# Spectral layer on one core: one subtraction, one set of stores, the exponentials and the interleaves of a spectrum placed elsewhere

## Chip, core and metric

The kernel runs on one core of one Trainium2 chip. The metric is device time in microseconds (us) of one execution, given as the median of several runs. Engines are named as in the profile: PE is TensorE, DVE is VectorE, ACT is ScalarE, POOL is GpSimd and SP is SyncE, which here only issues DMAs. Every engine works through its own queue in order.

## What is computed

The input x is 16 images of 16 channels, 256x256, fp32. Layer 0 normalises it by groups, applies a pole-residue operator (a convolution through the 2-D Fourier transform plus a transient part made of exponentials) and adds the result to x. Layer 1 normalises again, applies an involution network with a 3x3 convolution, and gates. The change touches layer 0 alone:

```python
alpha = jnp.fft.fft2(x, axes=(-2, -1))                   # x here is the normalised input
A = 1.0 / (omega1[:, None, None, None] - weights_pole1[None])
Bm = 1.0 / (omega2[:, None, None, None] - weights_pole2[None])
S = jnp.einsum('ikpq,oikp,xikq->oxik', weights_residue, A, Bm)
output_residue1 = jnp.einsum('biox,oxik->bkox', alpha, S)
C = jnp.einsum('biox,oikp->bikpx', alpha, A)
D = jnp.einsum('bikpx,xikq->bikpq', C, Bm)
output_residue2 = jnp.einsum('bikpq,ikpq->bkpq', D, weights_residue)
x1 = jnp.fft.ifft2(output_residue1, s=(Ny, Nx), axes=(-2, -1)).real
E1 = jnp.exp(weights_pole1[..., None] * tyc)             # complex exponentials
E2 = jnp.exp(weights_pole2[..., None] * txc)
F = jnp.einsum('kbpq,bipz->kbiqz', output_residue2, E1)
x2 = jnp.einsum('kbiqz,biqx->kizx', F, E2).real
return x1 + x2 / Nx / Ny
```

## The kernel before

Four stages run one after the other: `layer0_forward`, `layer0_mix`, `layer0_back`, `layer1`. Intermediate arrays go through DRAM: `al` (the spectrum), `hd`, `zn` and tables `td`, `avd`, `ed`.

**Forward** takes 64 steps, one for each image b and each group cg of four channels. `fetch` (L156) loads four planes `z` (1 MB) on SP, takes their statistics on DVE (L166, L168), and forms the even part (a sum, L172, DVE) and the odd part (a difference, L171, POOL) of the two halves of each image. `halves` (L175) applies the norm and folds the other axis (L185 to L191, DVE); `group_norm_scalars` sits between, with small DVE steps and a square root on ACT (L46). `rows` (L195) multiplies on PE by the Fourier matrix (L204) and by the pole table `at` (L211); ACT evicts (L218, L223). `poles` (L226) multiplies by the table `bt` (L233), and DVE and POOL accumulate (L244, L257 to L259). `columns` (L294) transforms the other axis for the image before: two PSUM tiles of matmuls (L305), two ACT evictions into a tile `o` (L312), and four stores of `o` to `al` issued from POOL (L321), twice a step; `o` has two buffers. After the 64 steps the columns of the last image remain.

`at` and `bt` are built at the start by `table` (L120), each in two halves of eight channels, with two 3.3 us reciprocals on DVE in each half: `at` whole before the first `rows`, `bt` whole during step 0. `tables` (L377) builds three more tables for the later stages. It is a generator: the step loop calls `next(pieces)` at L352 and L360, and what is left runs after the loop (L361). Its last part (L507 to L543) makes the exponentials of both axes: for each axis and each pair of channels it scales the coordinate by the poles' imaginary parts (L520), reduces the angle, takes the sine on ACT (L528), scales by the real parts (L531), runs `exponential` (a polynomial on DVE, L829) over 128x512, multiplies both (L535), and stores to `ed` from SP. The real parts of one axis fill 64 partitions; here they stand twice.

In this stage only PE's order is that of the program text. The other queues are ordered when the program is built, from its readiness estimates, so table work is spread over the steps.

**Mix** has 33 groups g. All its compute engines run in the order of the text. Each group holds four rounds f of `columns` for the group before (PE L733, ACT L743, then DVE L746, L747, L752 and POOL L753) and `mix` (PE L698, reading the spectrum tile `alb`), and then eight `residues` (PE L679; evicted by ACT L690 and DVE L688 in turn) between three `turn`s (PE L714). `columns` of one round cannot start on PE before DVE has emptied its two PSUM tiles of the round before (L746, L747). The next spectrum is brought in eight pieces q: SP loads one into one of two buffers `alc` (L599), and `interleave` (L631) writes it on DVE into the single tile `alx` (L628, L629) and then lets SP load the next piece. When all eight are in, `ends` fixes two rows, and `place` (L649) copies `alx` to `alb` by four DMAs of 512 KB (L652) once the last `mix` has been done. `poles` (L663) runs in round 1. Pieces 2 to 7 are interleaved in rounds 0 to 2, two in each, `ends` follows in round 2, and pieces 0 and 1 of the group after come behind the last residues.

Of the kernel before, what the change touches and what calls it, by code (L numbers as in the profile page):

```python
# [71 lines left out]
def layer0_forward(ctx, tc, d, al, bd, tabs):  # L72
# [31 lines left out]
    op = ctx.enter_context(tc.tile_pool(name="fo", bufs=2))  # L104
# [9 lines left out]
    def table_inputs(axis):  # L114
        wx = ap.tile([P, 2, 3, P], F32, tag="wx", name="wx")
        nc.sync.dma_start(out=wx, in_=d["wx"])
        w = frequencies(nc, ap, d["ty" if axis == "1" else "tx"], kcol, [P, 2], f"w{axis}")
        return wx, w

    def table(axis, wx, w):  # L120

        t, planes = (at, (0, 1)) if axis == "1" else (bt, (1, 2, 0))
        for half in range(2):
            cols = slice(512 * half, 512 * half + 512)
            pr = ap.tile([P, 512], F32, tag="pr", name="pr")
            pi = ap.tile([P, 512], F32, tag="pi", name="pi")
            nc.sync.dma_start(out=pr, in_=d[f"p{axis}r"][:, cols].to_broadcast([P, 512]))
            nc.sync.dma_start(out=pi, in_=d[f"p{axis}i"][:, cols].to_broadcast([P, 512]))
            p2 = ap.tile([P, 512], F32, tag="p2", name="p2")
            nc.gpsimd.tensor_tensor(p2, pr, pr, ALU.mult)  # L130
            q = ap.tile([P, 2, 2, 512], F32, tag="q", name="q", bufs=2)
            for h in range(2):
                e, r = q[:, h, 1], q[:, h, 0]
                nc.vector.tensor_scalar(e, pi, -1.0, w[:, h : h + 1], ALU.mult, ALU.add)
                nc.vector.tensor_tensor(r, e, e, ALU.mult)
                nc.vector.tensor_tensor(r, r, p2, ALU.add)
                nc.vector.reciprocal(r, r)
                nc.vector.scalar_tensor_tensor(e, e, -1.0, r, ALU.mult, ALU.mult)
                nc.vector.scalar_tensor_tensor(r, pr, -1.0, r, ALU.mult, ALU.mult)

            for y in range(2):
                for out, terms in ((0, ((0, 0), (2, 1))), (1, ((0, 1), (1, 0)))):
                    ps = psx.tile([P, 512], F32, tag="px", name="aps")
                    for n, (trig, part) in enumerate(terms):
                        nc.tensor.matmul(
                            ps, lhsT=wx[:, y, trig], rhs=q[:, y, part], start=n == 0, stop=n == 1
                        )
                    dst = t[:, y, 8 * half : 8 * half + 8]
                    src = ps.rearrange("p (c m) -> p c m", m=64)
                    nc.scalar.copy(dst[:, :, planes[out]], src)  # L150
                    if out and len(planes) == 3:
                        nc.vector.tensor_scalar(dst[:, :, planes[2]], src, -1.0, None, ALU.mult)
# [3 lines left out]
    def fetch(b, cg):  # L156
# [5 lines left out]
        )  # L162
        mv = sm.tile([P, 2, 2], F32, tag="mv", name="mv")
# [7 lines left out]
        nc.gpsimd.tensor_tensor(parts[:, 1], z[:, :, 0], z[:, :, 1], ALU.subtract)  # L171
        nc.vector.tensor_tensor(parts[:, 0], z[:, :, 0], z[:, :, 1], ALU.add)  # L172
        return eo, mv
# [120 lines left out]
    def columns(b, g0, rsc):  # L294
# [23 lines left out]
        for k in range(min(2, n)):  # L318
            w = (n - k + 1) // 2
            for v in range(2):  # L320
                nc.gpsimd.dma_start(  # L321
# [6 lines left out]
    with tc.manual_schedule(engines={mybir.EngineType.PE}):  # L328
        args = table_inputs("1")
        fetched = [fetch(*steps[0]), fetch(*steps[1])]  # L330
        table("1", *args)
# [3 lines left out]
        for i, (b, cg) in enumerate(steps):  # L335
            now, following = ready, iter(())
# [11 lines left out]
            if i == 0:  # L348
                table("2", *table_inputs("2"))
                passing.close()  # L350
# [1266 lines left out]
```

## Time and profile before

| what | value |
|---|---|
| runs of the kernel before | 6137.18, 6151.72, 6154.14 us; median 6151.72 us |
| profiled execution | 6126.97 us, of which the span (first to last instruction) is 6125.2 us |
| busy over the span | PE 5614.2 us (92%), DVE 4802.4 us (78%), POOL 2928.5 us (48%), ACT 2264.7 us (37%) |
| forward | 0 to about 1230 us; steps in 60 to 1167 us, then the last image's columns |
| mix | about 1230 to 2365 us |
| back and layer 1 | the rest |

Times in the profile are counted from the start of the span. The page splits the span into 40 slices of 153 us each, so forward is the first eight digits of each row and mix the next seven or so. A row of the timeline gives start, duration, engine, line, operation, tiles written and read, and in brackets the engine's idle time before and what ended it. Consecutive DVE instructions overlap: 128x128 instructions of 0.38 us start 0.22 us apart. In rows of waits the columns are total us, how often, and the longest.

### The profile page before, as it was taken

The page shows a single profiled execution, that of the slowest core. Times are in us where ns is not written, and L with a number is a line of the kernel's source. Part 1 is how long each engine was busy: PE and PEld are TensorE (multiplying, and loading weights), DVE is VectorE, ACT ScalarE, POOL GpSimd, SP SyncE. Part 2 cuts the span into 40 slices and gives each one's busy share as a digit, 9 for nine tenths or more (in the row PEclk, how much of TensorE's full clock was granted, in tenths as well). Part 3 has the DMA queues.
Part 4 walks back from the last instruction along what each step waited for, and adds up shares of the span by engine and source line. Part 5 has one row for each costly group of instructions (what it writes and reads, how often), then busy time and mean ns, then how long its engine had stood idle before and what let it go on. Part 6 is the DMA issues. An engine that isn't in the chain of part 4 may idle for free.

```text
span 6125.2 us, 217025 instructions
## 1 busy us (share of the span) xinstructions
PE 5614.2 (92%) x94280; PEld 3210.1 (52%) x94280; DVE 4802.4 (78%) x9275; ACT 2264.7 (37%) x4076; POOL 2928.5 (48%) x4154
## 2 busy tenths in 40 slices
PE   6888888778888887999899999999999999999997
PEld 4788888756776766777633333333333333333332
DVE  8999998767777775888828777778777787777784
ACT  2333444434434443222233333333333433333332
POOL 2455555523333333666633554445544455544453
PEclk9999999889999999999989999999999999999998
DMA  3445444456556566999867888888888888888886
GB/s 94 138 139 149 140 134 132 123 182 197 183 184 196 186 195 210 323 326 328 294 180 229 269 266 250 251 279 276 266 245 246 262 275 272 264 246 249 276 268 230
DMA packets 814779, 1370.51 MB, mean 224 GB/s; under 512 B 140001, under 2 KB 629345, under 8 KB 798689
## 3 DMA queue, kind: packets, MB, share of 16 engines
q1 hardware_dynamic: 596480, 882.02, 45.5%
q0 software_dynamic: 217344, 474.61, 25.2%
q8 instruction: 741, 12.14, 0.8%
q14 instruction: 214, 1.75, 0.1%
HBM read 730.18 MB, written 556.47 MB: 210 GB/s over the span
## 4 chain that ended last, share of the span: by engine, by line
PE 62%; DVE 12%; DMA 3%; issue 2%; ACT 1%; POOL 1%; SPq 0%; DVEq 0%; ACTq 0%; POOLq 0%
PE pd L1166 15%; PE c2ps L1244 15%; PE c L1116 12%; PE ps L679 4%; PE ph L733 3%; PE pr L1144 2%; DVE planes L1235 2%; PE pt L714 2%; PE py L923 2%; PE pg L698 2%; PE py L924 2%; DMA alc<-al 2%; DVE zb L955 1%; DVE st L940 1%; DVE alx L628 1%
## 5 line engine op out<-in xcount | busy, mean ns | idle before, releaser
L1196 POOL DMA_DIRECT2D cf<-top x1152 | 667.9, 692 | 1151.9 <-DVE top L1183 1011.7
L1235 DVE TENSOR_TENSOR planes<-rows 128x1152 f32<-128x1152 f32 x960 | 1201.1, 1293 | 0.0
L1166 PE MATMUL pd<-wide,dw 32*32 32x512 f32 x27648 | 1029.7, 601 | 28.0 <-issue 13.7
L1125 ACT ACTIVATE bot<-c,b 128x512 f32<-128x512 f32 x576 | 364.9, 684 | 1445.8 <-PE c L1116 1091.4
L1116 PE MATMUL c<-z,w 18*64 18x512 f32 x13824 | 833.5, 602 | 16.9 <-DMA z<-zn 16.9
L1166 PEld LDWEIGHTS pd<-wide,dw 32*32 32x32 f32 x27648 | 446.7, 103 | 588.5 <-issue 449.8
L1181 DVE TENSOR_TENSOR t<-pd,r 128x512 f32<-128x512 f32 x576 | 357.6, 683 | 479.8 <-PE pd L1166 479.8
L1116 PEld LDWEIGHTS c<-z,w 18*64 18x64 f32 x13824 | 291.1, 132 | 533.9 <-issue 411.9
L753 POOL TENSOR_TENSOR h<-w 128x256 f32<-128x256 f32 x258 | 193.6, 750 | 641.0 <-DVE w L747 638.1
L1214 POOL DMA_DIRECT2D cf<-bot x720 | 394.9, 619 | 217.8 <-DMA cf<-top 100.5
L1244 PE MATMUL c2ps<-planes,c 128*32 128x512 f32 x3968 | 477.5, 598 | 0.0
L1183 DVE TENSOR_TENSOR top<-pd,t 128x512 f32<-128x512 f32 x576 | 357.7, 683 | 100.0 <-PE pd L1166 99.6
L936 POOL TENSOR_TENSOR x<-x,o 128x512 f32<-128x512 f32 x256 | 324.0, 1266 | 215.6 <-DVE o L935 214.2
L204 PE MATMUL pu<-fy,f 128*128 128x128 f32 x2048 | 408.5, 281 | 7.9 <-ACT u L218 7.9
L1341 POOL TENSOR_SCALAR o<-o,scale,mean 128x258 f32<-128x258 f32 x488 | 341.5, 707 | 151.2 <-DVE scale L1333 132.0
L321 POOL DMA_DIRECT2D al<-o x544 | 337.4, 627 | 128.1 <-ACT o L312 83.6
L211 PE MATMUL pv<-at,f 128*128 128x128 f32 x2048 | 397.5, 276 | 0.0
L733 PE MATMUL ph<-ix,yt 64*128 64x128 f32 x4128 | 320.9, 298 | 73.0 <-DVE w L747 65.2
L1133 ACT ACTIVATE wide<-c,b 128x512 f32<-128x512 f32 x576 | 365.0, 693 | 0.0
L305 PE MATMUL px<-wxn,u 128*128 128x128 f32 (+1 forms) x2176 | 313.5, 306 | 42.2 <-ACT tt L441 24.1
L688 DVE COPY s<-ps 128x1024 f32<-128x1024 f32 x132 | 161.7, 1225 | 233.5 <-PE ps L679 233.5
L733 PEld LDWEIGHTS ph<-ix,yt 64*128 64x128 f32 x4128 | 286.0, 205 | 108.0 <-issue 82.4
(240 smaller groups left out, 10468.6 us busy)
## 6 DMA issues: line engine op xcount, KB each, us to landing
rows<-cf SPq DMA_DIRECT2D x128, 2176.0 KB
cf<-top POOLq DMA_DIRECT2D x896, 112.0 KB, 5.7
cf<-bot POOLq DMA_DIRECT2D x336, 224.0 KB, 6.3
z<-zn SPq DMA_DIRECT2D x576, 129.0 KB
alb<-alx SPq DMA_DIRECT2D x132, 512.0 KB
zn<-zb SPq DMA_DIRECT2D x128, 516.0 KB
o<-zn SPq DMA_DIRECT2D x128, 516.0 KB
z<-in_x SPq DMA_DIRECT2D x64, 1024.0 KB
```

The costliest lines, as they stand in the source:

```text
L204: nc.tensor.matmul(pu[:, h, :, :, e].rearrange("p v g m -> p (v g) m"), lhsT=f[:, e, c, h], rhs=fy[:, e].rearrange("p (n m) -> p n m", m=2 ...
L211: nc.tensor.matmul(pv[:, a, h], lhsT=f[:, e, c, h], rhs=at[:, e, 4 * cg + c].rearrange("p l m -> p (l m)"), start=e == 0, stop=e == 1,)
L733: nc.tensor.matmul(ph[q][:, e, blocks], lhsT=yt[lanes, i].rearrange("p t k -> p (t k)"), rhs=ix[lanes, i].rearrange("p (b x) -> p b x", b= ...
L1116: nc.tensor.matmul(ps[half, a][to : to + 64], lhsT=w1[lanes, dx], rhs=self.z[lanes, c : c + 2, dx : dx + N], start=dx == 0, stop=dx == 2,)
L1125: nc.scalar.activation(self.bot[:, c : c + 2], ps[1, a].rearrange("p c (x e) -> p c e x", e=2)[:, :, ::-1], AF.Mish, bias=b1[1],)
L1133: nc.scalar.activation(self.feat[:, c : c + 2, 1 : N + 1], ps[0, a], AF.Mish, bias=b1[0])
L1166: nc.tensor.matmul(out[32 * k : 32 * k + 32], lhsT=dw[lanes, kernel, dx], rhs=self.feat[lanes, 2 * k : 2 * k + 2, dx : dx + N], start=dx == 0,
L1183: nc.vector.tensor_tensor(self.top[:, s, half], out, t, ALU.add)
L1196: nc.gpsimd.dma_start(out=rows[y + 2 * lo : y + 2 * hi, :, c + 2 * k : c + 2 * k + 2].rearrange("y f c x -> y f (c x)"), in_=o[32 * k + 2 ...
L1214: nc.gpsimd.dma_start(out=rows[y + 4 * lo : y + 4 * hi, to : to + n].rearrange("p c x -> p (c x)"), in_=src.rearrange("p c q x -> p (c q x)"),
L1235: nc.vector.tensor_tensor(planes[:, k, rows], x[:, rows], y[:, rows], op_)
L1244: nc.tensor.matmul(ps[32 * j : 32 * j + 32], lhsT=w[:, blk], rhs=src[:, 4 * j + blk : 4 * j + blk + 4], start=(i, blk) == (0, 0), stop=(i, ...
```

## The change

1. Forward, `fetch`: the difference L171 goes from POOL to DVE. The load of `z` becomes a function of its own, `bring`, called at the top of a step for two steps ahead instead of at its end.
2. Forward, `columns`: the four stores a tile go from POOL to SP; `o` gets three buffers instead of two.
3. Forward, `table`: called by halves. Half 0 of `at` comes before the first step, half 0 of `bt` in step 0, both halves 1 in step 2. `wx` is loaded once instead of twice.
4. `tables`, exponentials: one `exponential` of 128x512 for both axes and two channels (axis 1 in partitions 0 to 63, axis 2 in the others), so 8 instead of 16. ACT makes its arguments and a copy with the halves exchanged; ACT also scales the angles (formerly L520). The product with the sine is done by halves of 64 partitions, for axis 2 together with the scale `last` (formerly L534). 24 pieces instead of 32.
5. Mix, `spread`: two instructions of 128x256 instead of four of 128x128 for a piece.
6. Mix, order: pieces 0 and 1 come behind residues 4 and 5, pieces 2 and 3 behind the last residues, 4 in round 0, 5 and 6 in round 2, 7 and `ends` in round 3, ahead of that round's copy L806.

`layer0_back` and `layer1` are not touched (`exponential` gets a parameter for a buffer's tag).

```diff
-    op = ctx.enter_context(tc.tile_pool(name="fo", bufs=2))
+    op = ctx.enter_context(tc.tile_pool(name="fo", bufs=3))
...
-    def table(axis, wx, w):
+    def table(half, axis, wx, w):
 
         t, planes = (at, (0, 1)) if axis == "1" else (bt, (1, 2, 0))
-        for half in range(2):
-            cols = slice(512 * half, 512 * half + 512)
...
+        cols = slice(512 * half, 512 * half + 512)
...
-    def fetch(b, cg):
+    def bring(b, cg):
 
         z = xp.tile([P, 4, 2, N], F32, tag="z", name="z")
         nc.sync.dma_start(
             out=z.rearrange("p c h x -> p (c h) x"),
             in_=d["x"][b, 4 * cg : 4 * cg + 4].rearrange("c (h p) x -> p (c h) x", p=P),
         )
+        return z
+
+    def fetch(z):
+
...
-        nc.gpsimd.tensor_tensor(parts[:, 1], z[:, :, 0], z[:, :, 1], ALU.subtract)
         nc.vector.tensor_tensor(parts[:, 0], z[:, :, 0], z[:, :, 1], ALU.add)
+        nc.vector.tensor_tensor(parts[:, 1], z[:, :, 0], z[:, :, 1], ALU.subtract)
         return eo, mv
...
-                nc.gpsimd.dma_start(
+                nc.sync.dma_start(
                     out=al[g0 // 2 + k, :, v, :, b, :w].rearrange("h c g x -> h c (g x)"),
...
-        args = table_inputs("1")
-        fetched = [fetch(*steps[0]), fetch(*steps[1])]
-        table("1", *args)
+        w1 = table_inputs("1")
+        wx = load(nc, ap, d["wx"], [P, 2, 3, P], "wx")
+        zs = [bring(*steps[0]), bring(*steps[1])]
+        table(0, "1", wx, w1)
+        fetched = [fetch(zs.pop(0)), fetch(zs.pop(0))]
+        w2 = table_inputs("2")
...
         for i, (b, cg) in enumerate(steps):
             now, following = ready, iter(())
+            if i + 2 < len(steps):
+                zs.append(bring(*steps[i + 2]))
+            if i == 2:
+                table(1, "1", wx, w1)
...
-            if i == 0:
-                table("2", *table_inputs("2"))
+            if i in (0, 2):
+                table(i // 2, "2", wx, w2)
+            if i == 2:
                 passing.close()
...
             if i + 2 < len(steps):
-                fetched.append(fetch(*steps[i + 2]))
+                fetched.append(fetch(zs.pop(0)))
...
+    for k in range(0, C, 2):
+        grown = tp.tile([P, 2, N], F32, tag="grown", name="grown")
+        for j in range(2):
+            for i, tr in enumerate(trs):
+                own = slice(64 * i, 64 * i + 64)
+                nc.scalar.activation(
+                    grown[own, j], tr[own], AF.Copy, scale=pr[own, k + j : k + j + 1]
+                )
+        exponential(nc, tp, grown.rearrange("p k x -> p (k x)"), "arg")
+        other = tp.tile([P, 2 * N], F32, tag="exp_n", name="other").rearrange("p (k x) -> p k x", k=2)
+        nc.scalar.copy(other[64:], grown[:64])
+        nc.scalar.copy(other[:64], grown[64:])
+        yield
+        for i in range(2):
...
             for j in range(2):
-                nc.vector.tensor_scalar(arg[:, j], tr, pi[:, k + j : k + j + 1], None, ALU.mult)
+                nc.scalar.activation(arg[:, j], trs[i], AF.Copy, scale=pis[i][:, k + j : k + j + 1])
...
-            yield
-            for j in range(2):
-                nc.vector.tensor_scalar(arg[:, j], tr, pr[:, k + j : k + j + 1], None, ALU.mult)
-            exponential(nc, tp, af)
-            if axis == "2":
-                nc.vector.tensor_scalar(n, n, last, None, ALU.mult)
-            nc.vector.tensor_tensor(arg, arg, n, ALU.mult)
-            if axis == "1":
+            for a, e in ((i, grown), (1 - i, other)):
+                own = slice(64 * a, 64 * a + 64)
+                if i:
+                    nc.vector.scalar_tensor_tensor(
+                        arg[own], n[own], last[own], e[own], ALU.mult, ALU.mult
+                    )
+                else:
+                    nc.vector.tensor_tensor(arg[own], n[own], e[own], ALU.mult)
+            if i == 0:
...
-        for h in range(2):
-            a, b = src[:, :, h, 0], src[:, :, h, 1]
-            nc.vector.tensor_tensor(dst[:, :, h, 0], a, b, ALU.add)
-            nc.vector.tensor_tensor(dst[:, :, h, 1], b, a, ALU.subtract)
+        a, b = src[:, :, :, 0], src[:, :, :, 1]
+        nc.vector.tensor_tensor(dst[:, :, :, 0], a, b, ALU.add)
+        nc.vector.tensor_tensor(dst[:, :, :, 1], b, a, ALU.subtract)
...
         alx = new_spectrum()
-        for q in range(2):
+        for q in range(4):
             interleave(alx, q)
...
-                if more and f < 3:
-                    for q in (2 + 2 * f, 3 + 2 * f):
+                if more:
+                    for q in ((4,), (), (5, 6), (7,))[f]:
                         interleave(alx, q)
-                    if f == 2:
+                    if f == 3:
                         ends(alx)
...
-                    if f == 3 and g + 2 < NF:
-                        for q in range(2):
+                    if f >= 2 and g + 2 < NF:
+                        for q in (2 * f - 4, 2 * f - 3):
                             interleave(alx, q)
```

## The prediction

> **What bounds it now.** I read the row of busy tenths first, then sums by stage, then the waits of forward, then single steps in the timeline.
>
> ```profile
> DVE  8999998767777775888828777778777787777784
> PEclk9999999889999999999989999999999999999998
> ```
>
> DVE is full through the first six slices, which are forward. The sums by stage (engine busy us, then clock, DMA share, GB/s):
>
> ```profile
> core 0: us, PE busy (x) PEld busy (x) DVE busy (x) ACT busy (x) POOL busy (x), PEclk, DMA share, GB/s
> 100.00:1167.00 1067.00, 943.42 (x8694) 883.66 (x8693) 1004.06 (x2366) 446.17 (x748) 568.73 (x749) 0.96 0.47 134
> 131.60:161.90 30.30, 28.39 (x280) 26.81 (x277) 30.27 (x83) 11.98 (x21) 14.49 (x17) 1.00 0.47 140
> 1262.00:2330.00 1068.00, 933.39 (x28406) 750.69 (x28398) 802.61 (x2078) 431.10 (x695) 353.60 (x480) 0.96 0.59 188
> ```
>
> In the 62 forward steps from 100 to 1167 DVE works 94% of the time, and PE 88%. The third row is two steps almost without table work. In mix (fourth) PE leads, and no engine is full. Waits in forward:
>
> ```profile
> ACT gnr L46 <- DVE gnv L44: 144.1, 42, 6.4
> PE pd L233 <- ACT v L223: 76.1, 41, 4.9
> ACT o L312 <- DMA al<-o: 40.2, 14, 5.5
> ```
>
> ACT stands at L46 until DVE has the variance; L223 stands behind it in ACT's queue, and PE waits for L223. So DVE sets the pace, by way of ACT. And L312 waits for a free buffer `o` once an image. One step shows what holds DVE up:
>
> ```profile
> 513.79 2.84 DVE L50 TENSOR_TENSOR gnt<-gnr 128x2 f32<-128x2 f32 x1
> 514.23 2.37 POOL L171 TENSOR_TENSOR eo<-z 128x1024 f32<-128x1024 f32 x1
> 516.55 0.28 DVE L485 TENSOR_TENSOR ar<-ar,tpr 128x128 f32<-128x128 f32 x1
> ```
>
> A two-element-wide DVE op (0.15 us elsewhere) lasts 2.84 us and ends as POOL's difference ends: DVE stands still for the whole of L171.
>
> **Difference to DVE.** L171 goes: 64 x 2.37 = 152 us in which DVE is held. Added: 64 x 1.22 (L172's median, same shape) = 78. Net -74 if DVE is always held. At the other end only two lines' excess counts: L50 64 x (0.73 - 0.15) = 37, L172 64 x (1.69 - 1.22) = 30, so 67 - 78 = +11. Other two-input lines have long ones too (L845 up to 3.86 against 0.69), so I take -70.
>
> The Trainium skill (Perfetto Trace Analysis, Optimizing Scalar/DVE Operations) says that a saturated DVE may be relieved by giving work to Scalar or even GPSIMD, which speaks against this edit; it adds that those two share a read port, so that this might not help. By the first half alone DVE would get 78 us more and forward would grow by about that; the rows above show the second half.
>
> **Exponentials.** One `exponential` takes 9.0 us of DVE (its 14 instructions where they ran alone, 1185.7 to 1195.2). Eight fewer: -72. L520 and L531 go to ACT: 16 x 2 x 0.62 = -20. L534 goes: 8 x 0.48 = -4. L535 becomes two of half the partitions, each as long (0.69): +11. Net -85. Some 8 of it lie behind 1167, so -77 in the steps. ACT gets 8 x (8 x 0.375 + 2 x 0.59) = 33 us (L743's 128x256, L718's 128x512), and it is idle over half the time. But each pair of channels now has six places where ACT, in order, waits for low-priority DVE work, against two before. 24 more, at 0.5 us (L528 waited 8.2 us in 16) to 3 us: 12 to 72 us on ACT, with evictions L218 and L223 behind. PE sees part of it: I take 17.
>
> **The 62 steps.** DVE after: 1004 - 70 - 77 = 857. PE: 943 busy less at most 4% of 1067 lost to the clock (0.96), 900. So PE becomes the bound. In the two plain steps PE was busy 28.39 of 30.30, 0.937: 900 / 0.937 = 960, a gain of 107, less 17 = **-90**. Bounds: -164 - 3 (PE never waits) and -25 (the difference gains nothing and ACT's new waits eat most of the rest).
>
> **Stores on SP, third buffer.** 8.5 stores a step leave POOL (0.63 us each, hidden there already) for SP, at 0.33 (table store L497) to 0.77 us (L652): 3 to 7 us of a 15 us step, SP being nearly empty. They now stand in order with loads of `z` and stores of `td`, `avd`, `ed`, which wait for DVE; before, they stood behind POOL's sums, which also wait for DVE. Behind a late one stand L312, then L218; three buffers cover 1.5 steps. Loads of `z` come a step early, so little waits for them. I cost this at nothing; the 40 us of L312's waits are inside the -90.
>
> **After the steps.** From 1167 to the last landing at about 1228 the last image's 17 evictions wait for stores again and again, and one left-over exponential sits among them.
>
> ```profile
> 1167.00:1262.00 95.00, 46.06 (x507) 37.28 (x509) 44.51 (x75) 20.54 (x29) 37.52 (x49) 0.72 0.54 171
> 1181.06 0.68 ACT L312 ACTIVATE o<-px,rsc 64x512 f32<-64x512 f32 x1 [6.51 <-DMA al<-o]
> 1212.78 1.27 ACT L312 ACTIVATE o<-px,rsc 128x512 f32<-128x512 f32 x2 [5.86 <-DMA al<-o]
> ```
>
> 61 us now. With 73 pieces (81 before) against 80 calls, none is left over. 8.25 tiles of 512 KB at mix's 188 GB/s are 23 us, PE's part 17, and a landing 5 more: 28 to 36. **-25** (-5 to -33).
>
> **Tables by halves.** The work stays; PE may run steps 1 and 2 (21 us between 99.5 and 120.5) while DVE makes the second halves, but DVE is 93% busy from 15.6 to 99.5. Between 0 and -21: **-12**.
>
> **Mix, spread.** Merging looks like a saving of two instructions' overhead, but rows of both shapes exist:
>
> ```profile
> 1244.90 0.58 DVE L628 TENSOR_TENSOR alx<-first 128x256 f32<-128x256 f32 x1
> 1245.33 0.59 DVE L629 TENSOR_TENSOR alx<-first 128x256 f32<-128x256 f32 x1
> 1261.29 0.38 DVE L628 TENSOR_TENSOR alx<-alc 128x128 f32<-128x128 f32 x1 [8.87 <-DMA alb<-alx]
> 1261.51 0.38 DVE L629 TENSOR_TENSOR alx<-alc 128x128 f32<-128x128 f32 x1
> ```
>
> Starts lie 0.43 and 0.22 us apart: a piece is 0.87 or 0.88. Nothing.
>
> **Mix, order.** One group now, about 35.0 us on average, 35.6 here:
>
> ```profile
> 1717.92 4.96 DMA alc<-al
> 1724.71 1.87 DVE L663 TENSOR_TENSOR lt<-av,m 128x512 f32<-128x512 f32 x3
> 1727.39 0.46 PE L733 MATMUL ph<-ix,yt 64*128 64x128 f32 x2 [2.59 <-DVE w L747]
> 1728.06 3.55 PE L733 MATMUL ph<-ix,yt 64*128 64x128 f32 x30 [0.20 <-DVE w L747]
> 1733.59 4.62 SPq L652 DMA_DIRECT2D alb<-alx  x4
> 1734.21 0.69 DVE L806 COPY y<-pg 128x512 f32<-128x512 f32 x1
> ```
>
> In round 1 DVE waits for pieces 4 and 5 (a pair of loads takes 5.0 us), then makes L663, and only then L747, for which PE waits 2.6 us. That stall goes. A new one comes. Count from L806, when the copy to `alb` is also issued. Residue 5 is copied by 9.0 (1.95 to the first DVE residue copy, twice 2.92, 1.23). Piece 0 needs `alx` free: 8.8 (1252.49 to 1261.29) to 10.4 us (median by the packets). Pieces 0 and 1 end at 10.8 to 12.2; the load for piece 2 starts after piece 0 and lands at 14.8 to 16.2; pieces 2 and 3 end at 16.6 to 18.0; the four L746/L747 (1.32) at 17.9 to 19.3. Only then can PE start round 1, which starts at 16.5 now (1715.16): **+1.4 to +2.8**. From there to the next L806 it is 19.05 now. New: round 3 starts on PE after 9.5 (four PE pieces of 1.95, two small waits); L752, pieces 5 and 6, one POOL clash, L746/L747, L752, piece 7, `ends` take 7.0, and 1.5 more if piece 7's load is late: 16.5 to 18.4, **-2.6 to -0.7**. Together -1.2 to +2.1 against this group, some 0.6 more against the mean: +1.0 x 32 = **+32** (-19 to +86).
>
> After the 2.6 us stall the clock was half from 1727.9 to 1731.3, and the next 1.98 us of matmul took 3.55. I leave that inside both sums, as the new stall is about as long. The Trainium skill (TensorE: Matmul & The Clock Gate, Part 1) wants an idle window of about 3.4 us for the lower clock; by it stalls this short would cost none, 1.6 us a group less, an estimate of some 50 us for the stage.
>
> **Sum.** -90 - 12 - 25 + 32 = -95. The profiled execution, 6127.0, becomes 6032. The median, 6151.7, lies 25 above it; the same on top gives **6057**.
>
> **Rivals.**
> 1. *PE-bound throughout* (0.13): forward's steps reach PE's 900 us, the stall in mix merely moves. -164 - 15 - 28 + 0 = -207: 5945. For it: two steps without columns have PE busy 19.9 of 21.0 us. Against: normalisation still crosses three engines a step.
> 2. *The queues take it back* (0.15): ACT behind the new exponential steps or SP behind table stores keeps DVE's old pace. -30 - 5 - 20 + 20 = -35: 6117. For it: L46's 144 us show how ACT's order costs PE. Against: three buffers, and half of ACT free.
> 3. *Slower* (0.14): the chain `alb` copy, piece 0, load, piece 2 in mix. With the copy at 10.4, the load at 5.0 and one POOL clash, round 1 starts at 20.3, +3.8; if late piece 7 also eats the gain behind it, 32 x 3.8 = +122, against a forward at its poor end, -60 - 5 - 25 = -90: +32, 6184. It decides from a loss of 2.8 us a group at that forward. Against: round 3's stall does go.
> My forecast has 0.58, its own range 5990 to 6125.
>
> **Chances.** Measurement cannot tell less than 0.3%, 18 us. Faster: 0.58 + 0.13 + half of rival 2 = 0.78; same 0.08; slower 0.14. Range 5975 to 6150.
>
> **What would show it.** Right: in forward DVE near 88% busy, PE near 92%, no DVE op of 2 us and more, steps of 15.8 us on average (977 / 62; 17.2 now); the time from the last step to `alb`'s memset near 36 us; in mix PE waiting for L747 in round 1 instead of round 3, and DVE waiting for `alc` ahead of piece 2. Wrong: ACT waiting for L846 or L527 by tens of us, SP waiting long with L312 waiting for `al<-o`, or groups of mix over 37 us.

## Result, and the profile after

The changed kernel takes 6169.78 us (median of 12 runs, 6154.98 to 6190.41), the kernel before 6152.32 us on the same chip (12 runs). The ratio is 1.0035, with a 95% interval of 1.0018 to 1.0051: about 21 us slower, where 95 us less had been forecast. The profiled execution takes 6178.25 us (span 6176.5), 51 us more than the profiled one of before. More than half of that is chance: the execution profiled before lies 25 us under its median, this one 8 us over its own.

The rows of busy tenths of the changed kernel, then its sums by stage (columns as in the prediction). The first stage runs from the second of the 64 steps to the end of the last. The prediction calls this stretch 62 steps; it holds 63 (2016 of the 2048 matmuls of L204, 32 a step).

```profile
DVE  8878778377777775888827777788777787777784
PEclk9999999899999998999989999999999999999998
```

```profile
core 0: us, PE busy (x) PEld busy (x) DVE busy (x) ACT busy (x) POOL busy (x), PEclk, DMA share, GB/s
67.70:1171.70 1104.00, 971.85 (x8734) 902.13 (x8732) 878.10 (x2324) 499.81 (x840) 110.38 (x189) 0.95 0.40 130
1171.70:1264.40 92.70, 41.16 (x479) 33.13 (x477) 22.25 (x25) 19.69 (x28) 9.07 (x5) 0.77 0.42 151
1264.00:2406.00 1142.00, 954.18 (x29312) 758.93 (x29312) 875.19 (x1637) 446.52 (x718) 382.36 (x496) 0.96 0.58 182
```

VectorE has been relieved as intended: 878 us busy in the 63 steps instead of 1004. Yet the steps take 1104 us instead of 1068, TensorE is busy for 88% of them as before, and the clock is no better. So something that is no engine's own work holds them. The waits in the 63 steps say where to look:

```profile
DVE st L167 <- DMA z<-in_x: 134.9, 44, 7.1
ACT gnr L46 <- DVE gnv L44: 101.6, 32, 6.7
PE gn_var L42 <- DVE gnq L39: 75.0, 30, 4.5
```

VectorE, which waited 10 us in all for the loads of `z` before, now waits 135 us for them. What stands behind the statistics in its queue is late, so L46's wait is still there, and TensorE now waits 75 us for the variance (11.5 before). The step that the prediction looked at (VectorE's timeline):

```profile
517.79 1.22 DVE L172 TENSOR_TENSOR eo<-z 128x1024 f32<-128x1024 f32 x1
518.92 1.22 DVE L173 TENSOR_TENSOR eo<-z 128x1024 f32<-128x1024 f32 x1
520.93 0.15 DVE L50 TENSOR_TENSOR gnt<-gnr 128x2 f32<-128x2 f32 x1
531.63 2.47 DVE L167 BATCH_NORM_STATS2 st<-z 128x6 f32<-128x512 f32 x4 [4.80 <-DMA z<-in_x]
```

L50 has gone from 2.84 to 0.15 us, and the difference L173 costs its 1.22 us. Ten us later VectorE stands still for 4.8 us because `z` has not landed. By the packets a load of `z` takes 7.5 us from issue to last packet (median), against 5.0 before. Its first packet ends 1.1 us after the issue in both kernels, and seven eighths of its packets have ended after 5.4 us (4.4 before): it is the tail that comes late. After the rows, ScalarE's timeline shows one eviction of `o` after another:

```profile
1203.80 1.27 ACT L313 ACTIVATE o<-px,rsc 128x512 f32<-128x512 f32 x2 [3.80 <-DMA al<-o]
1209.02 1.27 ACT L313 ACTIVATE o<-px,rsc 128x512 f32<-128x512 f32 x2 [3.95 <-DMA al<-o]
1214.09 1.27 ACT L313 ACTIVATE o<-px,rsc 128x512 f32<-128x512 f32 x2 [3.80 <-DMA al<-o]
```

A tile of 512 KB leaves every 5.1 us, although there are three buffers now. The view of the DMA queues, from 1196 to 1224 us (packets and rate; then queue, packets, MB, share of 16 engines):

```profile
DMA packets 1477, 2.87 MB, mean 102 GB/s; under 512 B 87, under 2 KB 87, under 8 KB 1475
...
q1 hardware_dynamic: 1475, 2.84, 26.2%
```

With nothing else to do, the stores move 102 GB/s and use 26.2% of sixteen engines, that is 4.2. The stretches of the profiled pair add up: the second step starts 31.8 us earlier (67.7 instead of 99.5), the steps take 36.0 more, the time from the last matmul of the rows to the first copy into `alb` 7.6 more (92.6 instead of 85.0), mix's 32 groups 31.6 more, and the rest, which is not touched, 7.8 more.

### The profile page after: what moved, and what is told of

Read it like the earlier page. It is cut to its first block, busy times and chain, and to the rows that moved or that the text cites. A ratio compares the mean times of both kernels' runs of the same rounds, so it can differ in the third digit from the quotient of the medians.

```text
span 6176.5 us, 216287 instructions
## 1 busy us (share of the span) xinstructions
PE 5616.6 (91%) x94280; PEld 3210.0 (52%) x94280; DVE 4678.7 (76%) x8643; ACT 2310.8 (37%) x4158; POOL 2451.4 (40%) x3546
## 4 chain that ended last, share of the span: by engine, by line
PE 51%; DVE 8%; issue 1%; DMA 1%; POOL 1%; ACT 0%; SPq 0%; DVEq 0%; ACTq 0%; POOLq 0%
PE pd L1193 15%; PE c2ps L1271 15%; PE c L1143 12%; PE pr L1171 2%; DVE planes L1262 2%; PE py L950 2%; PE py L951 2%; DVE zb L982 1%; DVE st L967 1%; PE pf L939 1%; DVE o L962 1%; DVE top L1210 0%; DVE o L961 0%; PE gn_mean L34 0%; ACT odd L959 0%
## 5 line engine op out<-in xcount | busy, mean ns | idle before, releaser
L1193 PE MATMUL pd<-wide,dw 32*32 32x512 f32 x27648 | 1033.3, 600 | 30.4 <-issue 15.5
L780 POOL TENSOR_TENSOR h<-w 128x256 f32<-128x256 f32 x258 | 210.3, 815 | 669.4 <-DVE w L774 663.3
L205 PE MATMUL pu<-fy,f 128*128 128x128 f32 x2048 | 430.5, 294 | 5.0 <-ACT u L219 5.0
L212 PE MATMUL pv<-at,f 128*128 128x128 f32 x2048 | 417.8, 288 | 0.0
L706 PE MATMUL ps<-tt,lt 64*32 64x256 f32 x8448 | 297.5, 405 | 111.7 <-DVE y L833 78.1
L725 PE MATMUL pg<-alb,s 128*32 128x64 f32 x16896 | 284.5, 222 | 67.0 <-issue 47.1
L205 PEld LDWEIGHTS pu<-fy,f 128*128 128x128 f32 x2048 | 334.0, 205 | 7.0 <-ACT u L219 5.9
L212 PEld LDWEIGHTS pv<-at,f 128*128 128x128 f32 x2048 | 333.0, 204 | 0.0
L306 PE MATMUL px<-wxn,u 128*128 128x128 f32 (+1 forms) x2176 | 289.6, 291 | 47.7 <-ACT o L313 31.2
```

Of the source, the lines that this page charges most:

```text
L205: nc.tensor.matmul(pu[:, h, :, :, e].rearrange("p v g m -> p (v g) m"), lhsT=f[:, e, c, h], rhs=fy[:, e].rearrange("p (n m) -> p n m", m=2 ...
L212: nc.tensor.matmul(pv[:, a, h], lhsT=f[:, e, c, h], rhs=at[:, e, 4 * cg + c].rearrange("p l m -> p (l m)"), start=e == 0, stop=e == 1,)
L1193: nc.tensor.matmul(out[32 * k : 32 * k + 32], lhsT=dw[lanes, kernel, dx], rhs=self.feat[lanes, 2 * k : 2 * k + 2, dx : dx + N], start=dx == 0,
```

## Experiments

Four questions: which part of the change takes forward's gain away; is it SyncE's queue or the engines that its stores run on; what is each other term worth; and what costs in mix. The table gives, from each profiled execution, the start of the second step, the length of the 63 steps from there on, TensorE's and VectorE's share in them, the time from the last matmul of the rows to the first copy into `alb`, and the mean group of mix. Ratios are to the kernel before on the same chip. A single profiled execution can lie well off its kernel's median (before 25 us under it, e3 20 and e7 13 us over), so differences of 10 or 20 us between profiles alone show little.

| kernel | median us | ratio, 95% | second step | 63 steps | PE, DVE | after the rows | group |
|---|---|---|---|---|---|---|---|
| before | 6152.32 | 1 | 99.5 | 1068.0 | .88, .94 | 85.0 | 34.98 |
| changed | 6169.78 | 1.0035, 1.0018 to 1.0051 | 67.7 | 1104.0 | .88, .80 | 92.6 | 36.03 |
| e1_stores_pool | 6068.32 | 0.9881, 0.9860 to 0.9903 | 67.5 | 1023.7 | .92, .86 | 70.6 | 35.90 |
| e2_mix_old | 6153.99 | 1.0016, 1.0003 to 1.0029 | 67.6 | 1085.2 | .89, .81 | 92.6 | 35.63 |
| e3_only_stores_sp | 6178.73 | 1.0060, 1.0038 to 1.0082 | 101.9 | 1088.9 | .87, .86 | 102.9 | 35.55 |
| e4_stores_pool_mix_old | 6062.48 | 0.9862, 0.9842 to 0.9882 | 66.5 | 1014.2 | .92, .87 | 73.5 | 35.78 |
| e5_z_on_pool | 6184.73 | 1.0051, 1.0034 to 1.0068 | 66.4 | 1105.3 | .88, .80 | 91.6 | 36.35 |
| e6_stores_by_16 | 6498.61 | 1.0558, 1.0535 to 1.0581 | 67.0 | 1389.6 | .75, .66 | 121.3 | 36.09 |
| e7_only_sub_dve | 6077.57 | 0.9885, 0.9866 to 0.9904 | 101.5 | 1005.5 | .93, .88 | 83.3 | 35.61 |
| e8_only_mix_new | 6185.52 | 1.0063, 1.0044 to 1.0082 | 99.1 | 1071.5 | .88, .94 | 85.1 | 36.31 |
| e9_sp_c_first | 6026.36 | 0.9810, 0.9792 to 0.9828 | 68.7 | 981.2 | .94, .90 | 66.2 | 35.94 |
| e10_sp_c_first_mix_old | 6018.32 | 0.9799, 0.9782 to 0.9816 | 68.0 | 976.3 | .94, .91 | 64.6 | 35.88 |
| e11_exp_old | 6077.58 | 0.9893, 0.9875 to 0.9911 | 67.7 | 1024.7 | .93, .89 | 83.7 | 35.91 |
| e12_only_sp_c_first | 6059.83 | 0.9856, 0.9835 to 0.9877 | 100.2 | 985.7 | .93, .95 | 74.0 | 35.42 |
| e13_mix_new_copy_first | 6148.60 | 1.0009, 0.9998 to 1.0021 | 99.2 | 1070.2 | .89, .94 | 88.2 | 35.41 |
| e14_sp_c_first_copy_first | 6019.21 | 0.9801, 0.9781 to 0.9822 | 69.1 | 979.4 | .94, .90 | 64.7 | 36.06 |

### Which part takes the gain

Two parts of the change were undone, alone and together, and one was made alone in the kernel before.

```diff
 e1, e4 (in the changed kernel)
-                nc.sync.dma_start(
+                nc.gpsimd.dma_start(
                     out=al[g0 // 2 + k, :, v, :, b, :w].rearrange("h c g x -> h c (g x)"),
 e2, e4 (in the changed kernel: mix's old order)
-        for q in range(4):
+        for q in range(2):
...
 e3 (in the kernel before)
-                nc.gpsimd.dma_start(
+                nc.sync.dma_start(
```

> The changed kernel with its spectrum stores (al<-o) issued from GpSimd again; the third buffer o stays. Theory A (the stores on SP are what eats forward's gain: they run on 4 of the 16 DMA engines at 102 GB/s, and the loads of z stand behind them in one queue, 8.0 us instead of 5.0 from issue to last packet, so that DVE waits 135 us for z): the waits of DVE for z fall under 30 us, the last rows matmul of forward comes at 1060 to 1100 us instead of 1172, the time from there to the first copy to alb falls from 93 to 60 to 70 us; in all 90 to 140 us less than the changed kernel, ratio to the kernel before 0.98 to 0.99. Rival B (ACT's new exponential steps and the fixed order of DVE's queue hold forward up): within 25 us of the changed kernel.

> The changed kernel with the old places of the interleaves and of ends in mix (the merged spread stays). Theory A (the new order trades the stall in round 3 for a longer one in round 1): groups of mix return from 36.0 to 35.0 us, 33 us less in all, about 0.998 of the kernel before. Rival B (the 1.05 us a group are scatter or come from the merged spread): groups stay at 36 us, no change.

> The kernel before with one edit: the stores of al issued from SP; two buffers o as before. Theory A (4 engines, z behind the stores): DVE's waits for z rise from 10 to 60 us and more, the last columns take 20 us longer or more; 40 to 100 us slower than the kernel before. Rival B: no change beyond 15 us.

> Both of the first two: stores from GpSimd and the old order in mix, all else as in the changed kernel. If the two effects are independent the gains add: 125 to 170 us less than the changed kernel, 0.975 to 0.983 of the kernel before. Rival: forward's gain is lost to something else, 0.995 or more.

With the stores back on GpSimd the changed kernel is 1.5% faster (0.9881 against 1.0035), 80 us of it in the steps and 22 us after the rows. The move alone makes the kernel before slower by 0.6%, 18 us of it after the rows. So this one edit takes away all the gain, and more. Mix's old order is worth some 12 us in the changed kernel (1.0016 against 1.0035), where 33 or nothing had been expected, and with the stores on GpSimd no more than the intervals allow for (0.9862 against 0.9881); so e4 missed its range. One expectation for e1 failed too: VectorE's waits for `z` fall to 79.5 us, not under 30.

### The queue or the engines

Two explanations were left: the loads of `z` stand behind up to 1 MB of stores in SyncE's queue (A), or the stores occupy four engines of sixteen, which a load of `z` needs too (B).

```diff
 e5: the loads leave SyncE's queue
-        nc.sync.dma_start(
+        nc.gpsimd.dma_start(
             out=z.rearrange("p c h x -> p (c h) x"),
 e6: each store cut into four of 16 partitions
-                nc.sync.dma_start(
-                    out=al[g0 // 2 + k, :, v, :, b, :w].rearrange("h c g x -> h c (g x)"),
-                    in_=o[64 * k : 64 * k + 64, v, :w].rearrange("p g x -> p (g x)"),
-                )
+                for h in range(4):
+                    nc.sync.dma_start(
+                        out=al[g0 // 2 + k, h, v, :, b, :w].rearrange("c g x -> c (g x)"),
+                        in_=o[64 * k + 16 * h : 64 * k + 16 * h + 16, v, :w].rearrange("p g x -> p (g x)"),
+                    )
 e9, e12: same stores, other order of rows
-                u[:, :, :, : NF - 1, cg, c].rearrange("p h v g f -> p (h v) g f"),
+                u[:, :, :, : NF - 1, c, :, cg].rearrange("p h v g f -> p (h v) g f"),
...
-                        lhsT=u[:, h, part, g0 + j : g0 + j + m].rearrange("p n g c f -> p (n g c f)"),
+                        lhsT=u[:, h, part, g0 + j : g0 + j + m].rearrange("p n c f g -> p (n c f g)"),
...
-                    out=al[g0 // 2 + k, :, v, :, b, :w].rearrange("h c g x -> h c (g x)"),
+                    out=al[g0 // 2 + k, :, v, :, b, :w].rearrange("h c g x -> c h (g x)"),
```

> The changed kernel with one edit: the loads of `z` are issued by GpSimd, on its own queue; the stores of `al` stay on SyncE. Theory A (the shared queue: a load of `z` stands behind up to 1 MB of stores, so the statistics and then the variance come late): the load's time from issue to landing falls from 8.0 to about 5 us, VectorE's waits for `z` (135 us) fall to 20 to 80 us, the last matmul of the rows comes at 1090 to 1120 us instead of 1172, while the time from there to mix's first group stays at 88 to 105 us, because the stores are as slow as before: 6085 to 6115 us. Theory B (slow stores at 102 GB/s keep the buffers `o`, and so ScalarE, late; the queue of `z` does not matter): last matmul of the rows at 1150 to 1172, 6145 to 6170 us.

> The changed kernel with one edit: each store of `al` on SyncE is cut into four, one for each of the four h, so that the outermost dimension of each is 16 and not 4. The loads of `z` stay on SyncE behind them. If the outermost dimension of 4 is what holds the stores at 102 GB/s, a tile of `o` goes out in 2.5 to 3.5 us instead of 5.1, and the time from the last matmul of the rows to mix's first group falls from 93 to 68 to 78 us. Theory B (slow stores alone): the rows end at 1090 to 1110 too, 6065 to 6090 us. Theory A (the shared queue): the loads of `z` still stand behind the stores, which only take half as long: rows end at 1120 to 1150, 6105 to 6135 us. If the stores stay slow: 6165 us or more, as SyncE issues 34 instead of 8.5 stores a step.

> The changed kernel with `u`'s last dimensions turned, so that the rows of `o` come out with the sixteen (c) outermost and the four (h) innermost, and each store of `al` has 16 and not 4 as its outermost dimension. Queue, number of stores, bytes and packets stay: SyncE still issues them, ahead of the loads of `z`. Theory B (four lanes: the stores use a quarter of the DMA engines, and `z`, which needs all of them, waits for these four): a tile of `o` goes out in 2.5 to 3.5 us instead of 5.1, the rows end at 1085 to 1110 us instead of 1172, the time from there to mix's first group is 68 to 78 us instead of 93, and the whole takes 6060 to 6090 us. Rival (SyncE's order: issues wait behind one another, whatever the transfers take): rows at 1150 to 1175, 6145 to 6170 us.

> The kernel before with the stores on SyncE and with 16 as their outermost dimension (`u` turned): the step that the prediction cost at nothing, without its four lanes. With four lanes the same move alone took +36 us (6179). If the lanes are all that was wrong, SyncE's order costs nothing and GpSimd's queue gains nothing that shows: 6140 to 6165 us. If the kernels with stores on SyncE beat those with stores on GpSimd (6026 against 6068) because VectorE or `z` is freed of something, that shows here too: 6090 to 6135 us. If the move itself costs, whatever the lanes: over 6165 us.

e5 is no faster than the changed kernel, and above both ranges: the steps take 1105 us again. Its list of DMA issues (last number: median us from issue to landing) shows that another queue does not help a load:

```profile
z<-in_x POOLq DMA_DIRECT2D x60, 1024.0 KB, 8.8
```

So A falls as far as SyncE's queue goes. e5 is not a clean test, because its loads are issued behind GpSimd's own work; but the 8.8 us count from the issue. e6 did not answer, and missed every range: it replaced one bound by another. SyncE's timeline after the rows has 63 issues back to back, 0.49 us each, and 32 KB in 0.49 us is 67 GB/s:

```profile
1499.74 30.62 SPq L323 DMA_DIRECT2D al<-o  x63
```

e9 keeps queue, number, size and packets of the stores, and makes the sixteen the outermost dimension instead of the four. For that `u` is turned, and with it the rows of `gc` (two loads, not shown); ScalarE's copy into `u` becomes dearer by it, 1075 ns instead of 582. Line numbers from `gc` on are 5 higher. ScalarE's timeline after the rows, the view of the DMA queues from 1058 to 1081 us, and the sum over the 63 steps:

```profile
1074.81 1.27 ACT L318 ACTIVATE o<-px,rsc 128x512 f32<-128x512 f32 x2 [1.92 <-DMA al<-o]
1077.35 1.27 ACT L318 ACTIVATE o<-px,rsc 128x512 f32<-128x512 f32 x2 [1.28 <-DMA al<-o]
```

```profile
DMA packets 2766, 4.45 MB, mean 193 GB/s; under 512 B 560, under 2 KB 688, under 8 KB 2763
...
q1 hardware_dynamic: 2731, 4.35, 55.9%
```

```profile
68.70:1049.90 981.20, 922.81 (x8734) 859.47 (x8732) 883.25 (x2323) 604.48 (x840) 110.45 (x189) 0.99 0.44 147
```

A tile leaves every 2.5 us, 26.2% of the engines have become 55.9%, a load of `z` takes 5.0 us again, and VectorE waits 1.2 us in all for it. The steps take 981 us, and the clock is 0.99: of the 123 us that they are shorter than in the change, 49 are TensorE's busy time for as many matmuls (971.85 against 922.81), and the rest is its idle time. The kernel is 2.2% faster than the change (0.9810 against 1.0035), some 138 us for the order of two dimensions, and faster than either expectation had it.

So the order of the dimensions is the cause, and the packet records show by what. A packet of the stores takes 84 ns (median) in both kernels, so neither order makes a packet slower. In the change four or five of them are in flight 98% of the time (1196 to 1224 us), in e9 eight or more for 81% (1058 to 1081 us). The Trainium skill (DMA: Bandwidth & Descriptors, "Rules for kernel authors") states it: the outermost dimensions of a transfer's two access patterns set how many engines it gets, so an outermost dimension under 16 confines it to at most that many; 4 here. These runs agree for stores from SyncE. Issued from GpSimd the same pattern, with the four outermost, is not so confined: in e1 such stores keep 53.8% of the engines busy (1095 to 1125 us). So it was the move to SyncE that confined them.

Less is shown of how four busy engines become lost time inside the steps. That the tail of a load waits on these four fits the packets, but a slow load is not all of it: in e1 and e7, with the stores on GpSimd, a load takes 7.3 and 6.7 us too, and VectorE waits 79.5 and 77.5 us for `z`. What goes with the time of the steps is TensorE's wait for the variance: 75.0 us in the change, 24.9 in e1, 4.2 in e9. Why late loads reach TensorE more in one kernel than in another stays open.

e12 is the term that the prediction set at nothing, with all engines instead of four: alone, it makes the kernel before faster by 1.4%, 82 us in the steps, more than was expected, and at least as much as the difference alone (0.9856 and 0.9885; the intervals just overlap). Sums by stage of e12, then VectorE's group L50 and GpSimd's difference, in before and in e12, over 56 steps (count, then busy us and mean ns):

```profile
100.20:1085.90 985.70, 917.06 (x8702) 861.24 (x8700) 933.26 (x2357) 550.38 (x746) 317.48 (x249) 0.98 0.44 145
```

```profile
L50 DVE TENSOR_TENSOR gnt<-gnr 128x2 f32<-128x2 f32 x56 | 43.9, 784 | 0.1
L171 POOL TENSOR_TENSOR eo<-z 128x1024 f32<-128x1024 f32 x56 | 134.8, 2408 | 3.2 <-issue 1.7 <-DVE gnr L47 0.6
```

```profile
L50 DVE TENSOR_TENSOR gnt<-gnr 128x2 f32<-128x2 f32 x56 | 16.9, 301 | 0.3
L176 POOL TENSOR_TENSOR eo<-z 128x1024 f32<-128x1024 f32 x56 | 200.4, 3579 | 212.6 <-DVE f L190 148.5 <-issue 54.0 <-DVE gnr L47 10.1
```

With GpSimd's queue free of stores, the difference starts elsewhere in the step: it now waits for VectorE's L190 (148.5 us) and becomes longer itself, 3579 ns instead of 2408, while L50 on the normalisation's path falls from 784 to 301 ns and ScalarE's wait at L46 from 144 to 56 us. So it holds up VectorE's short operations less. That this is all of the 82 us was not tested.

### The other terms of forward

e7 makes one part of the change alone. e11 is e4 with a pass of exponentials for each axis, as before.

```diff
 e7 (in the kernel before)
-        nc.gpsimd.tensor_tensor(parts[:, 1], z[:, :, 0], z[:, :, 1], ALU.subtract)
         nc.vector.tensor_tensor(parts[:, 0], z[:, :, 0], z[:, :, 1], ALU.add)
+        nc.vector.tensor_tensor(parts[:, 1], z[:, :, 0], z[:, :, 1], ALU.subtract)
 e11 (in e4)
-        exponential(nc, tp, grown.rearrange("p k x -> p (k x)"), "arg")
...
+            exponential(nc, tp, af)
```

> The kernel before with one part of the change: the difference of the halves of `z` on VectorE instead of GpSimd, after the sum. The prediction had -70 us for it on VectorE (bounds -74 and +11), in steps that VectorE sets: 6070 to 6100 us, no operation of 2 us and more on VectorE in forward. Rival: VectorE was held only as far as two lines show, and gets 78 us of new work for 67: 6150 to 6165 us.

> The changed kernel with the stores back on GpSimd, mix's old order (6062 us) and the old making of exponentials, a pass for each axis. Left of the change: the difference on VectorE, the third buffer, the tables by halves, the merged spread. The prediction had -77 us for the exponentials in the steps, +17 for ScalarE's waits, and part of -25 after them. If VectorE still set the pace: 6110 to 6135 us. If TensorE is the bound once the difference has gone, as the kernel before with the difference alone suggests (TensorE 93% busy, VectorE 88%): 6065 to 6085 us, with the loss in the time after the rows, where a left-over exponential stands again.

The difference alone saves 62.5 us in the steps (1068.0 to 1005.5), and 76 us by the medians. TensorE is then busy for 93% of them and is the bound. So the exponentials have little left to give there: e4 against e11 is 10.5 us in the steps and 10.2 after the rows, 0.3% together (0.9862 against 0.9893). e11 against e7 shows the tables by halves, with the third buffer, the earlier load and the merged `spread`: the second step starts 33.8 us earlier, the rows end 14.6 us earlier, and the time after them is the same (83.7 and 83.3). So the third buffer is worth nothing there. The whole does not show the 14.6 us: 0.9893 against 0.9885.

### Mix

e8 is the new order alone in the kernel before; e10 the old order in e9; e13 and e14 keep the new order but put piece 7 and `ends` of round 3 behind the copy.

```diff
 e13 (in e8), e14 (in e9)
-                    for q in ((4,), (), (5, 6), (7,))[f]:
+                    for q in ((4,), (), (5, 6), ())[f]:
                         interleave(alx, q)
-                    if f == 3:
-                        ends(alx)
...
                     nc.vector.tensor_copy(dst[:, 32:], src[:, 32:])
+                if more and f == 3:
+                    interleave(alx, 7)
+                    ends(alx)
```

> The kernel before with one part of the change: mix's pieces 2 and 3 brought ahead of the next group, the others in rounds 0, 2 and 3. The prediction had +32 us (-19 to +86): 6175 to 6190 us by it. From the changed kernel with the old order (-16 us) and from the pair with stores on GpSimd (-6 us) I now expect +5 to +16 us: 6148 to 6168 us, one group 0.2 to 0.5 us longer, and TensorE's wait gone from round 3 and come back in round 1 and at the first residues.

> The last kernel with mix's old order of pieces, the one part that was measured to cost by itself (+31 us in the kernel before; -16 and -6 us when undone in the changed kernel and in the one with stores on GpSimd). If both hold: 6 to 30 us less than the last kernel, 6040 to 6075 us. Rival: the order costs only where the copy into `alb` is late, and nothing here: within 5 us of the last kernel.

> The kernel before with the change's order of pieces in mix (alone: +31 us, ratio 1.0063), but piece 7 and `ends` of round 3 behind VectorE's copy L806 instead of ahead of it. If the order costs because L679 waits for L806, which stands behind piece 7 and `ends` on VectorE (92 us of such waits in 29 groups, against 19 to 24 us with the old order), these waits fall to 10 to 30 us and 25 to 50 us come back: 6125 to 6160 us (ratio 0.996 to 1.001). Rival (the copy into `alb`, which is issued after `ends`, 0.7 us later now, is what ends a group): the waits for L806 go, waits for `alb` or at L698 take their place, 6170 to 6200 us (ratio 1.003 to 1.009).

> The changed kernel with 16 as the outermost dimension of the stores (6026 us, ratio 0.981), and in mix piece 7 and `ends` behind the copy L833. By the first theory 10 to 45 us less than without the second edit: ratio 0.974 to 0.9795. By the rival the same or slower: 0.981 to 0.987.

Alone the order costs 0.6% (31 us by the medians), which is the prediction's +32 and not the +5 to +16 expected after e2 and e4. From TensorE's instructions, its idle time in an average group can be summed by place; the third row is the wait between the first and the second of the eight `residues`:

| us a group, ahead of | before | changed | e8 | e13 | e9 | e14 |
|---|---|---|---|---|---|---|
| round 3's `columns` | 1.96 | 0.29 | 0.19 | 0.19 | 0.29 | 0.28 |
| round 1's `columns` | 0.05 | 1.08 | 1.00 | 1.62 | 1.01 | 1.33 |
| the second residues | 0.78 | 2.49 | 2.99 | 0.56 | 2.64 | 0.47 |
| the first `mix` | - | 0.16 | - | 1.22 | 0.11 | 1.56 |

Round 3's stall goes and round 1's comes, as forecast. The third row was not forecast. VectorE, then TensorE, at the end of round 3 in a group of the changed kernel:

```profile
1823.27 0.58 DVE L655 TENSOR_TENSOR alx<-alc 128x256 f32<-128x256 f32 x1
1823.70 1.12 DVE L656 TENSOR_TENSOR alx<-alc 128x256 f32<-128x256 f32 x1
1824.67 0.65 DVE L666 COPY ends<-alx 128x16 f32<-128x16 f32 x1
...
1825.66 0.68 DVE L833 COPY y<-pg 128x512 f32<-128x512 f32 x1
```

```profile
1826.40 1.96 PE L706 MATMUL ps<-tt,lt 64*32 64x256 f32 x32 [2.83 <-DVE y L833]
```

TensorE has done the last `mix` and the first residues and waits for the copy that empties the PSUM tile of that `mix`, while VectorE writes piece 7 and the two end rows first. TensorE's waits in mix, for e8 and for e13:

```profile
PE ps L679 <- DVE y L806: 92.1, 29, 4.7
...
PE ph L733 <- DVE w L747: 34.7, 82, 2.1
```

```profile
PE ph L733 <- DVE w L747: 54.7, 73, 2.1
...
PE ps L679 <- DVE y L804: 17.3, 26, 2.3
```

With the copy first its wait falls from 92.1 to 17.3 us, the group from 36.31 to 35.41, and of +31 us some 5 remain (1.0009 against 1.0063). So in the kernel before, that copy is the cause. In e14 the stall ahead of the second residues goes too, 2.64 to 0.47 us, but 1.5 us come back ahead of the first `mix`, which needs the copy into `alb`, issued only after `ends`. That is the rival, in part: the kernel is 0.1% faster than e9, inside the intervals and between the two expectations. e10 gains no more. Why undoing the order is worth only 7 to 12 us by the ratios in the changed kernels, and making it costs 31 alone, stays open. The group column has a hint: in e3, e7 and e12, whose mix is that of the kernel before, a group takes 35.42 to 35.61 us and not 34.98. So the profiled kernel before has unusually short groups, and some 14 to 20 of the pair's 31.6 us need not be the order's.

e10 and e14 have the lowest ratios, 2.0% under the kernel before and 2.3% under the change; e9's interval overlaps theirs.

## Why the prediction was wrong

The failed step is "Stores on SP, third buffer". It priced the stores by what their issue costs SyncE and by what waits behind a late one, found that "loads of `z` come a step early, so little waits for them", and ended: "I cost this at nothing". It never asked how fast the transfer itself would run. In the trace of before these stores had only run from GpSimd (171 GB/s with all other transfers in the stretch after the rows); nothing there showed them from SyncE, so the step needed a bound from both sides and got none. In the change they run at 102 GB/s on four engines. A step stores 1056 KB, 10.6 us of these four at that rate, and the load of `z` needs some 4 us of them too (5.0 from issue to last packet, of which 1.1 to the first): 14.6 of the 15.5 us that a step was to take (977 us over 63 steps), an estimate. Alone this is +36 us where it was to be 0 (e3); in the change it is some 138 us, by the ratios of e9. The zero was wrong on the other side too. The step calls the stores "hidden there already" on GpSimd; taken off it, on all engines, they give 82 us in the steps (e12).

Step by step:

- **What bounds it.** Right, but for the count: the 62 steps are 63, so its 17.2 and 15.8 us a step are 16.9 and 15.5; the sum works with the whole stretch and does not need the count. e7 gains 62.5 us in the steps by VectorE's relief alone. The 2.84 us of L50 was VectorE held by GpSimd, and it is 0.15 without.
- **Difference, -70.** Right in size (-62.5 in the steps, -76 by the medians).
- **Exponentials, -77 + 17.** Too much, as measured behind the difference: 10.5 us, where TensorE is already busy 93% of the time. The sum did not use these terms one by one but went to TensorE's bound, so this did no harm.
- **The steps, -90 (960 us and 17 for ScalarE).** In the change it is +36. With the stores on all engines it is -87 (981.2 us, TensorE 94% and VectorE 90% against 92 and 88), but that near hit is luck: with the stores left on GpSimd the rest of the change gives -44 (e1, 1023.7 us), and the other 42 come with the stores off GpSimd's queue (e9 against e1), which the prediction had at nothing. So the failed step stands behind the +36 and behind half of the -87.
- **After the steps, -25.** +8 in the change. With stores on GpSimd -14, of which the left-over exponential is about 10 and the third buffer nothing; with stores on all engines -19.
- **Tables by halves, -12.** The second step starts 32 us earlier, and the rows end some 15 earlier (e11 against e7), as forecast; but the whole is no shorter (0.9893 against 0.9885), so the gain is not shown.
- **Spread, nothing.** 128x256 pieces start 0.43 us apart as forecast (1823.27, 1823.70); no run changes it alone.
- **Mix's order, +32.** Right in size alone (+31 by the medians), half right in place; the profiled pair's +31.6 is in part chance. Round 3's stall went (-1.7 us a group) and round 1's came (+1.0, forecast +1.4 to +2.8). But from round 3 to the copy L806 the working counted a gain of 0.7 to 2.6, and there the second residues wait 1.7 us longer, for the copy behind piece 7 and `ends`. A smaller loss and a missed one made the right sum, which is luck.

Of the rivals the second had the right direction, the queues giving the gain back, but its mechanism, SyncE's order and ScalarE's queue, is what e5 and e9 speak against. The sign that the prediction named for itself, L312 waiting for `al<-o`, is what the profile shows after the rows; in the steps it waits only 4.9 us. The third, slower through mix's chain into `alb`, came nearest in number (6184 against 6170), and by chance: mix lost some 32 us and not 122, and forward was 36 us slower in the steps, not 60 faster.

## To carry to other kernels

When DMAs are moved to another queue, price the transfer and not only the issue: look at the outermost dimension of both sides, and whether it can still be spread over sixteen engines. Where a load gets slower though its issue has not moved, look at the engines that a neighbouring store shares with it; another queue did not help here. And when work is put ahead of a short copy in an engine's order, ask which PSUM tile the copy empties and who waits for that tile.

## What was not expected of the hardware

- Two orders of the same 128 KB store, with the same packets of 2048 B: 102 GB/s with the four outermost, 193 GB/s with the sixteen.
- Issuing has a rate of its own: 0.49 us for each 32 KB store back to back in e6. That made four times as many stores worse than four engines, 67 GB/s against 102.
- The same pattern with the four outermost was confined to about four engines from SyncE (26.2% of sixteen) and not from GpSimd (53.8% in e1).
- The stores taken from GpSimd, on all engines, gained 82 us in the steps although GpSimd's difference stayed (e12), while the difference alone gained 62.5 and both with the rest of the change 87: they are not to be added.
